# One product for the overflow rows of two grouped quads in a graph network kernel, and their rows summed in bfloat16 parts

## The chip, the cores and the metric

The kernel runs on 1 core of one Trainium2 chip. The metric is the device time of one execution in microseconds; the time before is 2061.96 us, the median of 3 runs (2057.36 to 2062.47).

## What is computed

One layer of a graph network over 6250 nodes of 128 features and 200,000 edges. `f_ij` holds 20 numbers for each edge, `f_ij_cutoff` one.

```
h    = relu(layernorm(x))                       # 6250 x 128
t    = h @ W_in
W_ij = (shifted_softplus(f_ij @ W_f1 + b_f1) @ W_f2 + b_f2) * f_ij_cutoff
x_ij = t[idx_j] * W_ij                          # 200000 x 128; idx_j = dst, sorted
out  = segment_sum(x_ij, idx_i, 6250)           # idx_i = src, in no order
y    = x + shifted_softplus(out @ W_o1 + b_o1) @ W_o2 + b_o2
```

Everything is float32. The time goes to the two large steps: the products that make `x_ij` for 200,000 edges, and the sum of its rows by `src`.

## The kernel before

**Quads.** The edges are cut into chunks of 128, and four chunks make a quad (512 edges); there are 391 quads. One iteration `i` of the main loop works on several quads in different stages. For quad `i-1` TensorE makes `W` (line 494 the bias, line 505 the product), `xg` (line 497, the gathered node rows) and for the quad after next `z` (line 313); ScalarE (ACT) takes exp and ln of z (lines 318 and 323) and scales xg into `xc` (line 510); VectorE (DVE) multiplies W by xc (line 520). This gives the 512 rows of `x_ij`.

**Two ways to sum rows by `src`.** For 223 *plain* and *listed* quads the rows are added to accumulators in HBM by indirect DMAs that add, issued from GpSimd's queue (POOL, line 582, `scatter`), 128 rows each. The tile that holds the rows, `s` (line 519), has four buffers; a quad's buffer is free again when its four scatters have landed. For 168 *grouped* quads TensorE does the sum. The quads 8, 10, 12, 14, 17, 19, 21, 23, ... are grouped (gaps 2, 2, 2, 3), so in nine iterations there are four grouped quads and five others. A grouped quad goes through these steps:

- line 520 writes its rows in float32 into `pt` (`part_new`, line 670, two buffers). `part_rem` (line 676, DVE, iteration q + 2) subtracts twice, so that `pt` holds three parts whose upper halves are bfloat16 (`high`); columns 384 to 386 hold three numbers of the row (`part_ext`, line 682, ACT).
- `perm_oh` (line 662, DVE, iteration q + 1) makes the one-hot matrix `pm` (two buffers), which places each edge into one of 16 groups of 32 slots by its `src`, or, where a group is full, into one of 64 *overflow* slots.
- `permute` (line 687, TensorE, four products `pq` of 128 slots with all 387 columns, each the sum over four chunks) brings the edges to their slots; `perm_out` (line 693, ACT) copies the result to `mst` in bfloat16. Where quad q + 4's iteration holds a unit product, all four are made in iteration q + 3; otherwise two in q + 3 and two in q + 4.
- After eight grouped quads (a round) the *unit product* `un` (lines 761 to 792) adds the rows by node in PSUM, 96 matmuls of 32 rows each, and DVE adds the result to `accT`.

**The overflow.** The 64 overflow slots of a quad are brought together by `over_pe` (lines 702 to 704): per chunk three matmuls of 128 to 131 columns, one for each bfloat16 part, added up in PSUM in float32, twelve matmuls for a quad. The first quad of a pair uses PSUM partitions 0 to 63, the second 64 to 127, each in a PSUM buffer of its own. `over_out` (line 710, ACT) copies the 64 rows to half of the float32 tile `mo` (two of them). When both quads of a pair are there, `over_idx` (line 718) reads each row's node number, `over_dg`, `over_row` and `over_eq` (lines 723, 731, 736) build the matrix `eq` that says which of the 128 rows belong to the same node, `over_sum` (line 741) multiplies it with `mo`, so that every row holds its node's sum, and one scatter adds the result `os` (line 758).

**Order.** Everything is written out by hand: each engine runs its instructions in the program's order. `at(i, point, fn, ...)` hangs a step on a point of iteration i (`L`, `D0`, `D1`, `A0`, `A1`, `DM`, `PE2`, `A2`, `D2`, `S`), and `run` calls them there. `over_pe` hangs on `PE2` behind the products `pq`, for q + 4 (q + 3 where q + 4 is a unit iteration). The PSUM buffers with the tag `B` (four) serve pq, po, the row and sum products, rank products and un. `full[i]` (line 1240) counts the steps in `PE2` that take such a buffer, and moves the copies of a plain quad forward where there are more than two.

**The end.** After the last scatter the accumulators are loaded, added to `accT`, and multiplied by the output weights (lines 1353 to 1430).

Of the kernel before, what the change touches and what calls it, by code (L numbers as in the profile page):

```python
# [7 lines left out]
F32 = mybir.dt.float32  # L8
BF16 = mybir.dt.bfloat16
# [4 lines left out]
ALU = mybir.AluOpType  # L14
# [6 lines left out]
P = 128  # L21
SC = 1024
SEG = 512
GRP = 16
CAP = 32
OVC = 64
# [12 lines left out]
PW = 387  # L39
# [15 lines left out]
def tile_gnn(ctx: ExitStack, tc: tile.TileContext, x, fB, cT, srcT, srcr, dstr, win_, wf1, wf2, bias, bo1c, wo1,  # L55
             wo2, consts, ident, cmap, out, n_edges):
    nc = tc.nc
# [18 lines left out]
    GN = NP // GRP  # L76
# [4 lines left out]
    mpq = sorted_quads(NQ)  # L81
    mpi = {q: n for n, q in enumerate(mpq)}
# [21 lines left out]
    cp = ctx.enter_context(tc.tile_pool(name="cp", bufs=1))  # L104
# [3 lines left out]
    wk = edge.enter_context(tc.tile_pool(name="wk", bufs=2))  # L108
# [41 lines left out]
    dropT = cp.tile([P, EP // P], BF16, name="dropT")  # L150
    mos = []
    for i in range(2):
        mo_ = cp.tile([P, 132], F32, name=f"mo{i}")
        mos.append(mo_)

    rowid = con[:, 0:1]
    wgt = con[:, 1:2]
# [190 lines left out]
    def plainq(q):  # L348
        return q not in mpi and not LB <= plain[q] < LE
# [192 lines left out]
    def s3_idx(q):  # L542
        if not plainq(q):
            return
        s = st[q]["s"]
        jf = sp_.tile([P, 4], F32, tag="jf", name="jf")
        g = plain[q] // 4
        if late.get("jg") != g:
            late["jg"] = g
            late["jd"] = sp_.tile([P, 16], F32, tag="jd", name="jd", bufs=2)  # L550
            n16 = min(16, 4 * NS - 16 * g)
            nc.vector.tensor_scalar(late["jd"][:, :n16], srcT_sb[:, 16 * g:16 * g + n16], trash, None,
                                    op0=ALU.subtract)
        k = 4 * (plain[q] % 4)
        jd = late["jd"][:, k:k + 4]
        nc.vector.scalar_tensor_tensor(jf, s[:, :, 128], wgt2, jd, op0=ALU.is_lt, op1=ALU.mult)
        st[q]["jf"] = jf
# [28 lines left out]
    mp = {}  # L586
# [79 lines left out]
    def high(t):  # L666
        return t.bitcast(BF16)[:, :, 1::2]
# [25 lines left out]
        nc.scalar.copy(mp[q]["ms", s][:, :PW], mp[q].pop(("q", s))[:, :PW])  # L693

    def over_pe(q):
        h = mpi[q] % 2 * OVC
        t = ps.tile([P, 512], F32, tag="B", name="po", bufs=4)
        o = t[h:h + OVC]
        for c in range(4):
            w = mp[q]["pm"][:, c, GRP * CAP:]  # L700
            pt = high(mp[q]["pt"][:, c:c + 1])[:, 0]
            nc.tensor.matmul(o[:, :P + 3], w, pt[:, 2 * P:PW], start=(c == 0), stop=False)  # L702
            nc.tensor.matmul(o[:, :P], w, pt[:, P:2 * P], start=False, stop=False)  # L703
            nc.tensor.matmul(o[:, :P], w, pt[:, :P], start=False, stop=(c == 3))  # L704
        mp[q]["po"] = t

    def over_out(q):
        h = mpi[q] % 2 * OVC
        mo = mos[mpi[q] // 2 % 2]
        nc.scalar.copy(mo[h:h + OVC, :P + 3], mp[q].pop("po")[h:h + OVC, :P + 3])  # L710

    def over_none(q):
        nc.vector.memset(mos[mpi[q] // 2 % 2][OVC:, :P + 3], 0.0)

    def over_idx(q):
        mo = mos[mpi[q] // 2 % 2]
        so = sp_.tile([P, 1], F32, tag="ovs", name="ovs", bufs=3)
        nc.vector.scalar_tensor_tensor(so, mo[:, P + 2:P + 3], float(GN), mo[:, P + 1:P + 2], op0=ALU.mult, op1=ALU.add)
        mp[q]["so"] = so

    def over_dg(q):
# [10 lines left out]
        mp[q]["row"] = t  # L732

    def over_eq(q):
        eq = wk.tile([P, P], F32, tag="oeq", name="oeq", bufs=1)
        nc.vector.tensor_scalar(eq, mp[q].pop("row")[:, :P], mp[q]["so"], None, op0=ALU.is_equal)
        mp[q]["eq"] = eq

    def over_sum(q):
        t = ps.tile([P, 512], F32, tag="B", name="osum", bufs=4)  # L740
        nc.tensor.matmul(t[:, :P + 4], mp[q]["eq"], mos[mpi[q] // 2 % 2][:, :P + 4], start=True, stop=True)
        mp[q]["sum"] = t

    def over_copy(q):
# [91 lines left out]
    with tc.manual_schedule():  # L836
# [98 lines left out]
            nc.vector.tensor_copy(m_[:, :, 128:129], wgt.unsqueeze(1).to_broadcast([P, 4, 1]))  # L935
            ms.append(m_)
        for mo_ in mos:
            nc.vector.tensor_copy(mo_[:, P + 3:P + 4], wgt)
        idl = cp.tile([P, max(NW, 1)], F32, name="idl")
        iotl = cp.tile([P, P + LCAP], F16, name="iotl")  # L940
        nc.vector.tensor_scalar(iotl, iotw[:, GN // 2:GN // 2 + P + LCAP], float(LCAP - 1), None, op0=ALU.subtract)  # L941
# [7 lines left out]
        def at(i, point, fn, *a):  # L949
            hooks.setdefault((i, point), []).append((fn, a))  # L950

        def run(i, point):
            for fn, a in hooks.pop((i, point), []):
                fn(*a)

        at(1 if spread else 0, "D2", rel_ext, 0, rel0)
        if CE < EP // P:
            w = (CE + 4 * NS) // 2
# [145 lines left out]
        for t in range(0, NPT, 4):  # L1104
            i = mid + 8 * (t // 4) if spread else 0
            at(min(i + 9, NQ + 1), "D2", x_bias, t)
        r0_at = 0
        for g in range(len(tgroups)):
            i = clear(max(r0_at + 1, ret_at + 5), units)
# [4 lines left out]
        for r in range(-(-len(mpq) // RKQ)):  # L1114
            i = mpq[RKQ * r]
# [10 lines left out]
        for w in range((LE - LB) // SW):  # L1126
            for g in range(4):
                n = LB + SW * (w - 1) + 4 * g
                i = splain[n] + 2 if w else 6 + 2 * g
# [4 lines left out]
                i = clear(i + 2, units)  # L1134
# [4 lines left out]
            i = clear(i, units)  # L1139
# [4 lines left out]
            i = clear(i + 3, units)  # L1144
            at(i, "PE2", l_place, w)
            at(i + 1, "D0", l_take, w)
            i = clear(wend[w] + 12, units)
# [15 lines left out]
        for q in mpq:  # L1163
            at(q + 1, "D2", perm_oh, q)
            at(q + 2, "D2", part_rem, q, 1)
            at(q + 2, "D2", part_rem, q, 2)
            at(q + 2, "A2", part_ext, q)
            if q + 4 in units:
                for s in range(4):
                    at(q + 3, "PE2", permute, q, s)  # L1170
                for s in range(4):
                    at(q + 3, "PE2", perm_out, q, s)
                at(q + 3, "PE2", over_pe, q)
                at(q + 3, "PE2", over_out, q)
            else:
                for s in range(4):
                    at(q + 3 + s // 2, "PE2", permute, q, s)
                    at(q + 4 + s // 2, "A0", perm_out, q, s)
                at(q + 4, "PE2", over_pe, q)
                at(q + 5, "A0", over_out, q)  # L1180
            if q == mpq[-1] and mpi[q] % 2 == 0:
                at(q + 4, "D2", over_none, q)
            if mpi[q] % 2 or q == mpq[-1]:
                at(q + 5, "DM", over_idx, q)
                at(q + 6, "A0", over_dg, q)
                k = clear(q + 6, units)
                at(k, "PE2", over_row, q)
                at(k + 1, "D0", over_eq, q)
                k = clear(q + 8, units)
                at(k, "PE2", over_sum, q)  # L1190
                at(k + 1, "A0", over_copy, q)
                at(k + 1, "DM", over_ji, q)
                at(k + 1, "A2", over_int, q)
                at(k + 2, "S", over_scatter, q)
# [13 lines left out]
        for i in range(max(NQ + 7, last + 16, r0_end + 2, lend + 24)):  # L1208
            if i % 2 == 0 and i // 2 + 2 <= (NQ - 1) // 2:
                load_sc(i // 2 + 2)  # L1210
            run(i, "L")
            run(i, "D0")
            if i < NQ:
                s1_oh(i)
            run(i, "D1")
            if 0 <= i - 1 < NQ:
                s1_eq(i - 1)
            if 0 <= i - 1 < NQ:
                s2_pe_x(i - 1)
                s2_pe_w(i - 1)  # L1220
            if i + 1 < NQ:
                s1_pe(i + 1)
            if i < NQ:
                s1_exp(i)
                s1_ln(i)
            if 0 <= i - 3 < NQ and not full[i - 1]:
                s3_copy(i - 3, 0)
                s3_copy(i - 3, 1)
            run(i, "A0")
            if 0 <= i - 4 < NQ:  # L1230
                s3_ji(i - 4)
            run(i, "A1")
            if 0 <= i - 1 < NQ:
                s2_copy(i - 1)
            run(i, "DM")
            if 0 <= i - 1 < NQ:
                s2_m(i - 1)
            if 0 <= i - 3 < NQ:
                s3_idx(i - 3)
            full[i] = sum(fn in banked for fn, _ in hooks.get((i, "PE2"), [])) > 2  # L1240
            if 0 <= i - 2 < NQ:
                s3_pe(i - 2)
                if full[i]:
                    s3_copy(i - 2, 0)
                    s3_copy(i - 2, 1)
            run(i, "PE2")
            run(i, "A2")
            run(i, "D2")
            if 0 <= i - 4 < NQ and plainq(i - 4):
                s3_scatter(i - 4)  # L1250
            if 0 <= i - 2 < NQ and i - 2 not in mpi and not plainq(i - 2):
                s3_scatter(i - 2)
            run(i, "S")
# [26 lines left out]
    with tc.For_i(0, trips, 1) as ci:  # L1280
# [51 lines left out]
        eq = wk.tile([P, P], F32, tag="eq", name="feq", bufs=3)  # L1332
# [15 lines left out]
    pt = ctx.enter_context(tc.tile_pool(name="pt", bufs=2, space=PSUM))  # L1348
# [100 lines left out]
def sorted_quads(nq):  # L1449
    qs, q = [], MP0  # L1450
    while q < nq - MPEND:
        qs.append(q)
        q += MPGAPS[(len(qs) - 1) % len(MPGAPS)]
    return qs if len(qs) % RND <= EXTRA else qs[:len(qs) // RND * RND]
# [24 lines left out]
def clear(i, busy, n=1):  # L1479
    while any(i + k in busy for k in range(n)):  # L1480
        i += 1
    return i
# [113 lines left out]
```

## Time and profile before

| | |
|---|---|
| median of 3 runs | 2061.96 us (2057.36 to 2062.47) |
| the profiled execution | 2079.2 us, its span 2077.4 us |
| mean granted TensorE clock | 0.963 |
| TensorE busy | 1862.5 us (90%) |
| VectorE busy | 1659.4 us (80%) |
| GpSimd busy | 1643.9 us (79%) |
| ScalarE busy | 1482.8 us (71%) |
| po, lines 702 to 704 | 3 x 672 matmuls, busy 131.2, 127.2 and 127.3 us |
| pq, line 687 | 2688 matmuls, busy 533.0 us |
| scatters, line 582 | 987, of which 768 take 1.622 us on average |
| mo, line 710 | 168 copies of 0.262 us |
| osum, line 741 | 84 products, 168 float32 passes of 0.295 us |

The profile comes from one execution, recorded by the hardware profiler. Busy time is the time in which an engine has an instruction under way; TensorE's matmuls overlap, so that two of 0.22 us may start 0.06 us apart, and what a matmul costs is read from one start to the next. Behind the bar of a line of the profile stand the busy time, the mean duration of one instruction in ns, and the idle time before the group with what ended it. "issue" is a time in which the engine waited for nothing that the profile shows. POOL is GpSimd, PEld TensorE's weight loads.

### The profile page before, as it was taken

Reading aid. Unit: us, or ns where it says so; the run is one execution under the profiler, and the core shown is the slowest. Engines: PE = TensorE matmul, PEld = TensorE weight load, DVE = VectorE, ACT = ScalarE, POOL = GpSimd, SP = SyncE. Lnnn points to the kernel's source line nnn. Section 1 sums busy time; section 2 is a strip of 40 time slices with the busy share of each in tenths; the row PEclk is TensorE's granted clock in tenths of the full one; section 3 lists DMA queues with packets and bytes.
Section 4 is the critical chain, followed back from the end, with each engine's and each line's share of the span. In section 5 each row is a group of like instructions: output and inputs, shape, how many; then the busy total and the mean of one; then the engine's idle time right before and its main releaser. Section 6 shows DMA issues by size and latency. Waiting matters only on the chain. (4 is left out here: it accounts for less than half of the span.)

```text
span 2077.4 us, 57578 instructions
## 1 busy us (share of the span) xinstructions
PE 1862.5 (90%) x20381; PEld 1288.0 (62%) x20381; DVE 1659.4 (80%) x4448; ACT 1482.8 (71%) x4083; POOL 1643.9 (79%) x1040
## 2 busy tenths in 40 slices
PE   3579988899999999999999999999999999999956
PEld 2456666566666666666666666666666666677734
DVE  3678887797888888988988978979889788787635
ACT  2468776777776777777678777777877777788714
POOL 3578787888877888887878878888888888888774
PEclk9679999999999999999999999999999999999977
DMA  7887766667766766766667666676676676667648
GB/s 238 227 210 147 125 118 120 121 112 130 130 118 114 126 127 119 139 123 123 120 120 130 120 119 118 118 124 117 120 134 108 124 121 111 110 119 131 130 48 239
DMA packets 381188, 272.57 MB, mean 131 GB/s; under 512 B 97727, under 2 KB 341354, under 8 KB 380898
## 3 DMA queue, kind: packets, MB, share of 16 engines
q0 software_dynamic: 143728, 71.30, 35.2%
q1 hardware_dynamic: 236882, 197.50, 34.1%
q8 instruction: 161, 2.64, 0.5%
q14 instruction: 129, 1.06, 0.2%
q10 hardware_dynamic: 288, 0.07, 0.0%
HBM read 154.45 MB, written 114.24 MB: 129 GB/s over the span
## 5 line engine op out<-in xcount | busy, mean ns | idle before, releaser
L582 POOL DMA_INDIRECT acc<-s,lji x768 | 1245.7, 1622 | 266.6 <-issue 180.3
L687 PE MATMUL pq<-pt,pm 128*128 128x387 bf16 x2688 | 533.0, 341 | 44.6 <-DVE pt L676 10.6
L510 ACT ACTIVATE xc<-xg,cb 128x128 f32<-128x128 f32 x1564 | 446.4, 371 | 135.7 <-PE xg L497 119.9
L505 PE MATMUL W<-w,a 128*128 128x128 f32 x3128 | 464.1, 292 | 0.1
L505 PEld LDWEIGHTS W<-w,a 128*128 128x128 f32 x3128 | 388.4, 195 | 42.3 <-issue 3.1
L687 PEld LDWEIGHTS <-pm 128*128 128x128 bf16 x2688 | 260.3, 99 | 233.4 <-issue 37.2
L693 ACT CAST mst<-pq 128x387 bf16<-128x387 f32 x672 | 302.2, 481 | 135.0 <-PE pq L687 96.5
L781 PE MATMUL un<-so,mst 32*128 32x392 bf16 x8064 | 374.5, 327 | 17.3 <-DVE pr L627 7.0
L781 PEld LDWEIGHTS <-mst 32*128 32x128 bf16 x8064 | 227.8, 93 | 157.1 <-issue 60.2
L323 ACT ACTIVATE a<-a,con 128x512 f32<-128x512 f32 x391 | 282.3, 722 | 12.7
L582 POOL DMA_INDIRECT acc<-s,ji x123 | 200.2, 1628 | 80.4 <-issue 26.4
L318 ACT ACTIVATE a<-z 128x512 f32<-128x512 f32 x391 | 238.3, 610 | 26.8 <-PE z L313 17.2
L676 DVE TENSOR_TENSOR pt<-pt 128x512 f32<-128x512 f32 x336 | 231.8, 690 | 5.8
L662 DVE TENSOR_SCALAR pm<-iot,pos 128x576 bf16<-128x576 f16 x672 | 221.8, 391 | 0.0
L792 DVE TENSOR_TENSOR accT<-un,accT 128x392 f32<-128x392 f32 x320 | 158.6, 558 | 73.7 <-PE un L781 37.5
L520 DVE TENSOR_TENSOR s<-W,xc 128x512 f32<-128x512 f32 x192 | 131.9, 687 | 85.9 <-ACT xc L510 52.0
L766 DVE TENSOR_SCALAR so<-iot,mst 128x392 bf16<-128x392 f16 x672 | 191.0, 344 | 6.7 <-PE un L781 6.7
L582 POOL DMA_INDIRECT acc<-os,oji x96 | 156.4, 1629 | 31.2 <-issue 18.0
L497 PE MATMUL xg<-wn,oh 63*128 63x128 bf16 x1564 | 157.3, 222 | 15.8 <-ACT xc L510 9.4
L313 PE MATMUL z<-ft,ws 123*128 123x512 bf16 x391 | 152.0, 389 | 15.7 <-DVE iotl L941 9.4
L494 PE MATMUL W<-b2rep,onesb 64*128 64x512 bf16 x391 | 153.9, 394 | 0.0
L520 DVE TENSOR_TENSOR pt<-W,xc 128x512 f32<-128x512 f32 x168 | 115.2, 686 | 47.9 <-ACT xc L510 29.5
(209 smaller groups left out, 2435.5 us busy)
## 6 DMA issues: line engine op xcount, KB each, us to landing
rb<-reld SPq DMA_DIRECT2D x391, 64.0 KB
fsd<-f SPq DMA_DIRECT2D x49, 480.0 KB
ft<-fsd SPq DMA_DIRECT2D x195, 120.0 KB
sb<-src SPq DMA_DIRECT2D x169, 128.0 KB
fb<-in_fB_dram SPq DMA_DIRECT2D x49, 320.0 KB
ft<-fsd SPq DMA_DIRECT2D x195, 80.0 KB
wn<-tab SPq DMA_DIRECT2D x782, 15.8 KB
acc<-s,lji POOLq DMA_INDIRECT x768
```

The lines of the kernel that those rows point to most:

```text
L318: nc.scalar.activation(a, st[q]["z"], AF.Exp)
L323: nc.scalar.activation(a, a, AF.Ln, bias=half, scale=0.5)
L505: nc.tensor.matmul(W[:, c, :], st[q]["a"][:, c * P:(c + 1) * P], w2, start=False, stop=(c == 3))
L510: nc.scalar.mul(xc[:, c, :], st[q]["xg"][:, c, :], late["c", q // CQ][:, 4 * (q % CQ) + c:4 * (q % CQ) + c + 1])
L520: nc.vector.tensor_tensor(m[:, :, :P], st[q]["W"], st[q]["xc"], op=ALU.mult)
L582: nc.gpsimd.indirect_dma_start(out=accs[k][:rows, :], out_offset=bass.IndirectOffsetOnAxis(ap=ji, axis=0), in_=s, in_offset=None, compute_ ...
L662: nc.vector.tensor_scalar(pm[:, c], iot[:, :SLOTS], rk[r]["pos"][:, 4 * j + c:4 * j + c + 1], None, op0=ALU.is_equal)
L676: nc.vector.tensor_tensor(pt[:, :, k * P:(k + 1) * P], a, high(a), op=ALU.subtract)
L687: nc.tensor.matmul(t[:, :PW], mp[q]["pm"][:, c, s * P:(s + 1) * P], high(mp[q]["pt"][:, c:c + 1, :PW])[:, 0], start=(c == 0), stop=(c == 3))
L693: nc.scalar.copy(mp[q]["ms", s][:, :PW], mp[q].pop(("q", s))[:, :PW])
L766: nc.vector.tensor_scalar(so, iotw[:, :GN], w[:, 3 * P // 2:3 * P // 2 + 1], None, op0=ALU.is_equal)
L781: nc.tensor.matmul(ts[g][:, :GN], mp[q]["ms", s][v, k * P:(k + 1) * P], mp[q]["oh"][v], start=(q == qs[0] and k == 0), stop=(q == qs[-1] a ...
```

## The change

- `mo` becomes bfloat16 and holds the three parts side by side (387 columns, and a column with the row weight).
- `over_pe` handles both quads of a pair in one call: for each chunk one matmul of all 387 columns for the first quad into partitions 0 to 63, then one for the second into partitions 64 to 127, of the same PSUM buffer, eight matmuls for a pair.
- It hangs on a new point, `PE1`, in iteration q + 3 of the pair's second quad. `PE1` is run before the products of a plain quad and before `PE2`. `over_out` follows there: one copy of 128 rows with 387 columns. `over_none` goes into it.
- `over_idx` reads the two columns of `mo` in their new place, `eq` is bfloat16, and `over_sum` makes three matmuls, one for each part, in place of one in float32.
- `over_pe` no longer counts in `full`, since it isn't in `PE2`.
- The scratch memory for the descriptors of GpSimd's DMAs is set to 8192 bytes of a partition; nothing was set before, which means 16384.

In the order of TensorE's instructions the pair's eight products now stand right behind z (line 313) of their iteration. `pt` and `pm` keep two buffers each; those of a pair's first quad are now read until iteration q + 3 of the second.

```diff
-        mo_ = cp.tile([P, 132], F32, name=f"mo{i}")
+        mo_ = cp.tile([P, PW + 1], BF16, name=f"mo{i}")
...
     def over_pe(q):
-        h = mpi[q] % 2 * OVC
+        qs = mpq[mpi[q] // 2 * 2:mpi[q] + 1]
         t = ps.tile([P, 512], F32, tag="B", name="po", bufs=4)
-        o = t[h:h + OVC]
         for c in range(4):
-            w = mp[q]["pm"][:, c, GRP * CAP:]
-            pt = high(mp[q]["pt"][:, c:c + 1])[:, 0]
-            nc.tensor.matmul(o[:, :P + 3], w, pt[:, 2 * P:PW], start=(c == 0), stop=False)
-            nc.tensor.matmul(o[:, :P], w, pt[:, P:2 * P], start=False, stop=False)
-            nc.tensor.matmul(o[:, :P], w, pt[:, :P], start=False, stop=(c == 3))
-        mp[q]["po"] = t
+            for h, p in enumerate(qs):
+                nc.tensor.matmul(t[h * OVC:(h + 1) * OVC, :PW], mp[p]["pm"][:, c, GRP * CAP:],
+                                 high(mp[p]["pt"][:, c:c + 1, :PW])[:, 0], start=(c == 0), stop=(c == 3))
+        mp[q]["po"] = t, len(qs) * OVC
 
     def over_out(q):
-        h = mpi[q] % 2 * OVC
+        t, n = mp[q].pop("po")
         mo = mos[mpi[q] // 2 % 2]
-        nc.scalar.copy(mo[h:h + OVC, :P + 3], mp[q].pop("po")[h:h + OVC, :P + 3])
-
-    def over_none(q):
-        nc.vector.memset(mos[mpi[q] // 2 % 2][OVC:, :P + 3], 0.0)
+        nc.scalar.copy(mo[:n, :PW], t[:n, :PW])
+        if n < P:
+            nc.vector.memset(mo[n:, :PW], 0.0)
...
-        eq = wk.tile([P, P], F32, tag="oeq", name="oeq", bufs=1)
+        eq = wk.tile([P, P], BF16, tag="oeq", name="oeq", bufs=1)
...
     def over_sum(q):
         t = ps.tile([P, 512], F32, tag="B", name="osum", bufs=4)
-        nc.tensor.matmul(t[:, :P + 4], mp[q]["eq"], mos[mpi[q] // 2 % 2][:, :P + 4], start=True, stop=True)
+        mo = mos[mpi[q] // 2 % 2]
+        nc.tensor.matmul(t[:, :P + 4], mp[q]["eq"], mo[:, 2 * P:], start=True, stop=False)
+        nc.tensor.matmul(t[:, :P], mp[q]["eq"], mo[:, P:2 * P], start=False, stop=False)
+        nc.tensor.matmul(t[:, :P], mp[q]["eq"], mo[:, :P], start=False, stop=True)
...
                 for s in range(4):
                     at(q + 3, "PE2", perm_out, q, s)
-                at(q + 3, "PE2", over_pe, q)
-                at(q + 3, "PE2", over_out, q)
             else:
                 for s in range(4):
                     at(q + 3 + s // 2, "PE2", permute, q, s)
                     at(q + 4 + s // 2, "A0", perm_out, q, s)
-                at(q + 4, "PE2", over_pe, q)
-                at(q + 5, "A0", over_out, q)
-            if q == mpq[-1] and mpi[q] % 2 == 0:
-                at(q + 4, "D2", over_none, q)
             if mpi[q] % 2 or q == mpq[-1]:
+                at(q + 3, "PE1", over_pe, q)
+                at(q + 3, "PE1", over_out, q)
                 at(q + 5, "DM", over_idx, q)
...
                 s3_idx(i - 3)
+            run(i, "PE1")
             full[i] = sum(fn in banked for fn, _ in hooks.get((i, "PE2"), [])) > 2
...
-    nc = bacc.Bacc("TRN2", target_bir_lowering=False, num_devices=1)
+    nc = bacc.Bacc("TRN2", target_bir_lowering=False, num_devices=1, dynamic_dma_scratch_size=8192)
```

More of the change, by code (lines that the diff above doesn't have):

```diff
@@ L717, in over_idx @@
         so = sp_.tile([P, 1], F32, tag="ovs", name="ovs", bufs=3)
-        nc.vector.scalar_tensor_tensor(so, mo[:, P + 2:P + 3], float(GN), mo[:, P + 1:P + 2], op0=ALU.mult, op1=ALU.add)
+        nc.vector.scalar_tensor_tensor(so, mo[:, PW - 1:PW], float(GN), mo[:, PW - 2:PW - 1], op0=ALU.mult, op1=ALU.add)
         mp[q]["so"] = so
@@ L937, in tile_gnn @@
         for mo_ in mos:
-            nc.vector.tensor_copy(mo_[:, P + 3:P + 4], wgt)
+            nc.vector.tensor_copy(mo_[:, PW:PW + 1], wgt)
         idl = cp.tile([P, max(NW, 1)], F32, name="idl")
```

## The prediction

> **What bounds the kernel now.** I read the sums of the page first, then busy time by stretch for all engines, then who GpSimd waits for, then the timeline around one overflow product.
>
> ```profile
> PE 1862.5 (90%) x20381; PEld 1288.0 (62%) x20381; DVE 1659.4 (80%) x4448; ACT 1482.8 (71%) x4083; POOL 1643.9 (79%) x1040
> ```
>
> TensorE looks like the bound with 90%, GpSimd (POOL) like an engine with a fifth to spare. The stretches correct that; their columns are the stretch, its length, then busy time and instructions of PE, PEld, DVE, ACT, POOL.
>
> ```profile
> 119.10:330.00 210.90, 189.43 (x1927) 131.13 (x1925) 174.27 (x490) 159.69 (x449) 169.27 (x105) 0.96 0.75 143
> 330.00:1300.00 970.00, 904.76 (x10269) 620.18 (x10271) 822.98 (x2261) 726.87 (x2015) 792.50 (x487) 0.98 0.69 122
> 1300.00:1960.00 660.00, 635.72 (x7160) 441.49 (x7153) 543.74 (x1414) 509.07 (x1410) 552.81 (x344) 1.00 0.69 121
> 1960.00:2017.20 57.20, 40.70 (x530) 27.96 (x528) 28.78 (x84) 15.33 (x49) 46.15 (x30) 0.85 0.47 53
> ```
>
> POOL's instructions here are the row scatters of line 582, and before nearly every one the engine stands 0.30 us on "issue", which is no idleness that another engine could fill:
>
> ```profile
> POOL acc L582 <- issue: 112.3, 368, 0.3
> POOL acc L582 <- DVE s L520: 24.9, 12, 4.7
> POOL acc L582 <- DMA acc<-s,lji: 14.5, 42, 2.0
> ```
>
> (the waits of POOL between 330 and 1300 us). So a scatter occupies 1.62 us and 0.30 us of issue. From 1300 to 1960: 552.8 + 344 x 0.30 = 656 of 660 us. From 330 to 1300: 792.5 + 487 x 0.30 = 939 of 970. TensorE and POOL are both full; of the whole time from 119.1 to 2017.2 us POOL spends 1560.7 + 966 x 0.30 = 1850.5 us of 1898.1, and only 47.6 us on real waits. Of these 10 lie before 330 us (mostly for landed DMAs), 31 between 330 and 1300 (the 12 waits for s of line 520 give 24.9 - 12 x 0.3 = 21), 4 after that and 2 at the last stage. The tail starts from POOL's last scatter: it ends at 2017.1, the loads of the accumulators follow it, and the tail takes 60 us whatever happened before. TensorE is done at 2009.
>
> So **what TensorE saves is worth at most the time that POOL waits for it**, 31 + 4 + 2 less 2 us for landed DMAs (42 x 0.3 of their 14.5 us is issue): some 35 us.
>
> **What the overflow costs TensorE now.** One quad:
>
> ```profile
> 1233.92 0.34 PE L687 MATMUL pq<-pt,pm 128*128 128x387 bf16 x1
> 1234.19 0.25 PE L702 MATMUL po<-pt,pm 128*64 128x131 bf16 x1
> 1234.27 0.22 PE L703 MATMUL po<-pt,pm 128*64 128x128 bf16 x1
> 1234.33 0.22 PE L704 MATMUL po<-pt,pm 128*64 128x128 bf16 x1
> ...
> 1234.87 0.22 PE L704 MATMUL po<-pt,pm 128*64 128x128 bf16 x1
> 1235.02 0.39 PE L494 MATMUL W<-b2rep,onesb 64*128 64x512 bf16 x1
> ```
>
> Starts count here, since matmuls overlap: from the last pq to the next W 1.10 us. Where no po stands between (1229.43, eight pq of 0.34 within 1.57, W at 1230.93) it is 0.27. A quad's overflow costs 0.83 us, 168 quads 139 us. pq to pq is (1.57 - 0.34) / 7 = 0.17, pq to po 0.27: changing to 64 columns costs 0.10 on the way in, and I take as much on the way out.
>
> **What replaces it.** Eight products of 387 columns for two quads, the halves in turn, between z (line 313) and the next full product: 2 x 0.10 for the change of shape, and 0.17 for each product, 8 x 0.17 + 0.20 = 1.56 us, if one follows the other; 4 x 0.17 + 0.20 = 0.88 if the two halves run at once. No row of before shows two column halves at once. The nearest for it is the unit product, four groups of 32 rows at once:
>
> ```profile
> 1236.66 4.16 PE L781 MATMUL un<-so,mst 32*128 32x392 bf16 x96
> ```
>
> 96 products of 392 columns in 4.16 us are 0.043 us each, a quarter of 0.17. The nearest against it are the eight pq in a row. I take 0.88, because un is the row in which products of separate parts of the array alternate as here. A pair then saves 2 x 0.83 - 0.88 = 0.78 us, 84 pairs 65; at 1.56 it saves 0.10, 84 pairs 8.
>
> The weight loads (line 702, 0.11 us each for 64 columns) hide: in the fence of one quad the products start each 0.06 us, with a load each. If they stood bare, a product would cost 0.17 + 0.11, the pair 8 x 0.28 + 0.20 = 2.44 us, and TensorE would lose 0.78 x 84 = 66 us. The Trainium skill (TensorE: Matmul & The Clock Gate, Part 3) says that a weight load overlaps matmuls under way only when the row groups differ, and all eight here use all 128 rows: by that rule this loss is the outcome. The trace of before does not agree: its twelve steps of 0.06 us use the same rows throughout.
>
> *The sum over rows* (line 741): float32, two passes, 0.23 us from 1232.47 to the next pq at 1232.70; now three bfloat16 products of 128 to 132 columns at 0.06 = 0.18. 84 x 0.05 = 4 us saved.
>
> *The place.* The pair's product moves ahead, to iteration q + 3 of the second quad, right behind z. There it needs that quad's remainders (line 676, DVE), which are late in about half of the 84 places: at 1380.05 the two take until 1381.46, while z is done with its place at 1379.68. Before, only pq waited there (until 1381.52), and lcnt, osum or the rank products filled part of that time; now they stand behind the waiting po. Going through the timeline pair by pair, the late remainders cost at most 41 us in all, and what stood in their shadow is 20 to 25. I charge 20. Behind the waiting po on TensorE: the rank, row and sum products, pq and the next iteration.
>
> *The evacuation* (line 710): two of 0.262 us become one like line 693's, 0.481. ACT now waits for it before the next exp, up to about 1 us; exp and ln are needed an iteration (4.8 us) later, and that hides it. Its copies of the second pair of pq come later, though, into the iteration of a unit product, whose four tiles need those PSUM buffers: between nothing and 0.5 us, 42 times, 0 to 20 us; I take 5.
>
> *The second buffer.* pt of a pair's first quad now stays until iteration q + 3, and with two buffers the m of the quad after (line 520, DVE) has to wait for po in every other pair. In those places it starts 1.6 to 6.4 us after W, median 3.5, po ends 2.5 after W. So it costs nothing in most, and at most 1 us where it waits. The bfloat16 eq and the memset are within 0.1 us of what they replace.
>
> *The halved descriptor scratch* of GpSimd's DMAs: no row shows a wait for it. The two ends are the shortest scatter, 1.54 us, at which it costs nothing, and the longest, 2.54, at which 987 scatters cost 987 us; a gain would need a scatter under 1.54, and there is none. I take zero, because 643 of the 963 scatters after 119 us lie within 0.02 of the shortest. Each 0.01 us per scatter would be 10 us, for POOL has no slack to hide it.
>
> Sum on TensorE: 65 + 4 - 20 - 5 = 44 us saved, spread evenly: 23 of them between 330 and 1300 us, and some 5 before, against 29 us of waits on POOL there; after 1300 POOL waits 6 more. I take some seven tenths of the 35, because the waits come in lumps (10 us of them between 600 and 700), ahead of which TensorE has not yet won as much: **25 us**. What is late next is POOL; the rest of TensorE's saving turns into waits of line 520 for the scatter buffers s. The profiled execution took 2079.2 with a span of 2077.4, so its span becomes 2052; the median of the runs is 2062.0, 17 lower, and I subtract from that: 2037.
>
> **The rivals.**
> - *The halves run one after the other.* For it: no row shows the contrary. TensorE saves 8 + 4 and pays 20 + 5 for the place and the evacuation, 13 us lost; the half of it that falls between 330 and 1300 us makes POOL wait longer, the rest is in POOL's stock of rows (at 1810 us a listed quad's scatter starts 11 to 15 us after its line 520): some 2068, and 2054 to 2072 with the bounds of these costs.
> - *Slower: scatters wait for descriptor space.* Place: POOL, line 582. It decides as soon as a scatter takes 25 / 987 = 0.025 us more. The mean is already 0.08 above the shortest; as much again gives 79 - 25: 2116. Against it: most scatters follow each other at 1.54 + 0.30 us without any wait.
> - *Slower: weight loads bare.* TensorE loses 66 - 4 and 20 for the place, all of it on the path: some 2140. Against it: the steps of 0.06 us.
> - *More than POOL's waits:* scatters shorten too, because 74 us of their time is excess over 1.54. By the timeline line 676 (DVE) lies beside the 164 scatters over 1.7 us for 0.55 us on average and beside the others for 0.12; nothing removes it, but its place may shift. 2015 to 2022.
>
> **How the numbers follow.** Forecast (2022 to 2048) 0.65; one after the other 0.14, of which half is slower and a third within 0.3% (6 us, about what a measurement of this kernel can tell from no change); scratch 0.08; bare loads 0.04; more 0.04; unnamed 0.05. The range, 2022 to 2068, leaves out scratch, bare loads, more, and the top of the second case. Faster by over 0.3%: 0.65 + 0.02 + 0.04 less a little, 0.70; within: 0.10; slower: 0.20.
>
> **What would show it.** Right: po starts 0.09 apart on average, eight within 0.9 us; POOL's waits for s shrink from 25 us to a few, its sum of busy and issue reaches 99% from 330 us on; line 520 waits for landed scatters; the last scatter ends near 1992. Wrong: po starts 0.17 apart; mean of line 582 above 1.65 us; TensorE waiting for line 676 over 40 us in all, or un for line 693; POOL still waiting for s.

## The result, and the profile after

The changed kernel takes 2068.98 us (median of 10 runs, 2063.73 to 2075.84) against 2062.82 us (10 runs) of the kernel before beside it: a ratio of 1.0034, 95% interval 1.0018 to 1.0049. It is slower by a third of a per cent. The forecast was 2037 us, a gain, with a range of 2022 to 2068. In a later comparison on another chip (`a_again` below) the change lost 0.2%, and with three buffers (`v6`) as much. The profiled execution took 2067.92 us, its span 2066.1.

The sums of the profile, and busy time by the same stretches as before:

```profile
PE 1815.0 (88%) x19121; PEld 1190.5 (58%) x19121; DVE 1658.7 (80%) x4448; ACT 1468.1 (71%) x3999; POOL 1648.0 (80%) x1040
```

```profile
119.10:330.00 210.90, 186.86 (x1785) 119.33 (x1787) 173.86 (x489) 158.06 (x440) 171.42 (x106) 0.94 0.73 143
330.00:1300.00 970.00, 887.89 (x9683) 576.09 (x9672) 831.86 (x2295) 723.99 (x1988) 802.15 (x491) 0.98 0.67 123
1300.00:1960.00 660.00, 620.22 (x6713) 408.97 (x6716) 540.61 (x1399) 508.20 (x1390) 551.91 (x342) 0.99 0.67 122
```

Between 330 and 1300 us TensorE is busy 17 us less than before (887.9 against 904.8), and that is no gain: it is idle instead. The wait that stands out on TensorE after the change, and one on ScalarE (line, what it waited for, us in all, times, longest):

```profile
PE po L700 <- DVE pt L676: 63.3, 47, 4.0
```

```profile
ACT mo L707 <- PE po L700: 106.3, 83, 4.4
```

In an execution of the kernel before (the run `b_again` below) TensorE's wait for line 676 stood at its pq and was small, and ScalarE waited for single po of one quad, a little each time:

```profile
ACT mo L710 <- PE po L704: 30.2, 96, 0.9
...
PE pq L687 <- DVE pt L676: 9.7, 18, 1.3
```

ScalarE's figure varies between profiles: 106.3 us here, 76.2 in `a_again`, 64.0 in `v6`; TensorE's is 61 to 63 in all three.

One such place after the change, on TensorE, VectorE and ScalarE:

```profile
1238.63 0.38 PE L313 MATMUL z<-ft,ws 123*128 123x512 bf16 x1
1238.94 0.36 PE L700 MATMUL po<-pt,pm 128*64 128x387 bf16 x1
1240.37 0.86 PE L700 MATMUL po<-pt,pm 128*64 128x387 bf16 x7 [1.07 <-DVE pt L676]
1241.16 0.39 PE L612 MATMUL rkp<-G,tri 128*128 128x512 bf16 x1
```

```profile
1237.44 0.46 DVE L599 TENSOR_TENSOR G<-ge 128x512 bf16<-128x512 bf16 x1
1237.82 0.64 DVE L601 TENSOR_REDUCE cnt<-ge 128x32 f32<-128x480 bf16 x1
...
1238.90 1.42 DVE L676 TENSOR_TENSOR pt<-pt 128x512 f32<-128x512 f32 x2
```

```profile
1238.00 1.16 ACT L510 ACTIVATE xc<-xg,cb 128x128 f32<-128x128 f32 x4
1241.26 0.48 ACT L707 CAST mo<-po 128x387 bf16<-128x387 f32 x1 [2.10 <-PE po L700]
```

The first quad's product runs at 1238.94; the second's needs the remainders of line 676, which VectorE begins only after other work at 1238.90, and TensorE stands 1.07 us. ScalarE has reached its copy at 1239.16 and stands 2.10 us, and the next exp and xc stand behind it in its order. GpSimd's waits for the whole stretch from 119.1 to 2017.2 us, after the change:

```profile
POOL acc L582 <- issue: 235.3, 771, 0.4
POOL acc L582 <- DMA acc<-s,lji: 16.6, 46, 1.2
POOL acc L582 <- DVE s L520: 15.7, 14, 2.9
```

and in `b_again`:

```profile
POOL acc L582 <- issue: 227.3, 745, 0.3
POOL acc L582 <- DMA acc<-s,lji: 19.8, 55, 1.1
POOL acc L582 <- DVE s L520: 18.0, 15, 2.8
```

The wait for s that was to shrink to a few us is 15.7, against 18.0 in `b_again` (25.5 in the profile of the prediction): it has hardly changed.

### The profile page after: what moved, and what is told of

Same layout as the page of the kernel before. It is cut to its first block, busy times and chain, and to the rows that moved or that the text cites. A ratio compares the mean times of both kernels' runs of the same rounds, so it can differ in the third digit from the quotient of the medians.

```text
span 2066.1 us, 54971 instructions
## 1 busy us (share of the span) xinstructions
PE 1815.0 (88%) x19121; PEld 1190.5 (58%) x19121; DVE 1658.7 (80%) x4448; ACT 1468.1 (71%) x3999; POOL 1648.0 (80%) x1040
```

## The experiments

The runs stand in four groups, each on one chip of its own beside runs of the kernel before: the first four rows, the next four, then three and three. The kernel before took 2063.9, 2075.1, 2079.2 and 2077.4 us there, so times are compared within a group and only ratios from group to group. The ratio is to the kernel before. "No overflow scatters" and "line 676 a copy" leave out part of the work, so these runs say something of time alone.

| run | what | us | ratio (95%) |
|---|---|---|---|
| b_again | the kernel before | 2063.1 | 1.0000 (0.9984 to 1.0015) |
| b_scratch | before, scratch 8192 | 2063.1 | 1.0007 (0.9991 to 1.0023) |
| b_noos | before, no overflow scatters | 2043.9 | 0.9907 (0.9875 to 0.9939) |
| a_noos | changed, no overflow scatters | 2036.8 | 0.9882 (0.9849 to 0.9916) |
| v1 | changed, later place, pm two buffers | 2079.8 | 1.0024 (1.0005 to 1.0043) |
| a_lateout | changed, ScalarE's copy later | 2129.1 | 1.0267 (1.0240 to 1.0295) |
| a_copy | changed, line 676 a copy | 2051.3 | 0.9899 (0.9871 to 0.9927) |
| b_copy | before, line 676 a copy | 2061.1 | 0.9931 (0.9903 to 0.9958) |
| v6 | changed, three buffers | 2084.3 | 1.0019 (1.0005 to 1.0034) |
| v5 | v6 with the product moved | 2068.0 | 0.9949 (0.9931 to 0.9967) |
| v5_noos | v5, no overflow scatters | 2029.5 | 0.9768 (0.9745 to 0.9790) |
| a_again | changed | 2080.5 | 1.0021 (1.0006 to 1.0037) |
| b_again2 | the kernel before | 2076.5 | 1.0003 (0.9990 to 1.0016) |
| v5_again | v5 | 2066.5 | 0.9954 (0.9940 to 0.9968) |

**1. The kernel before once more, and its scratch.** `b_again` has no edit; `b_scratch` has one line:

```diff
-    nc = bacc.Bacc("TRN2", target_bir_lowering=False, num_devices=1)
+    nc = bacc.Bacc("TRN2", target_bir_lowering=False, num_devices=1, dynamic_dma_scratch_size=8192)
```

> The kernel before, unchanged, for a second profile: the first one's execution took 2079.2 us, 16 more than the median of its runs. Theory A (GpSimd's scatters are full in an ordinary execution, and the first profile shows waits that an ordinary one has not): the span is 2056 to 2066 and GpSimd's real waits (idle beyond 0.305 us before a scatter) from 119 us to the last scatter are about 30 us, as in the profile after (28), against 44 in the first profile. Theory B (the first profile is typical in this, and the change lost TensorE's saving to new waits): the waits are again 40 us or more.

> The kernel before with the descriptor scratch of GpSimd's DMAs at 8192 bytes, nothing else. Theory C (the smaller scratch makes the scatters longer, which is the loss of the change): mean of the list scatters 1.63 us or more against 1.62, and 4 to 10 us slower than before. Theories A and B: within 0.1% of before.

The scratch costs nothing that can be measured, so theory C falls (mean of a listed scatter 1.618 us, `b_again` 1.619). `b_again` shows how much one profile of the kernel before differs from the next: GpSimd's real waits after 119 us (each idle time less 0.305 us of issue) are 28.6 us at 2060.4 us, where the profile of the prediction had 44.0 at 2079.2. That is what theory A expected, on this chip; experiment 7 has a profile of the same kernel with 45.7.

**2. GpSimd relieved.** In both kernels the 84 scatters of the overflow rows are left out:

```diff
-    for q in mpq[1::2] + mpq[-1:] * (len(mpq) % 2):
-        scat[q + 10] += 1
...
-                at(k + 2, "S", over_scatter, q)
```

> The kernel before without the 84 scatters of the overflow rows (their sums are made but not added to the accumulators, so that part is missing in the output). GpSimd has 84 x 1.92 = 161 us less to do and is no longer full. Theory A: the time falls by 20 to 50 us and TensorE alone is the bound. If TensorE and the others were the bound already, it falls by less than 10.

> The changed kernel without the 84 scatters of the overflow rows (that part is missing in the output). Theory A: with GpSimd relieved, TensorE's saving shows: 25 to 45 us below the kernel before without these scatters. Theory B (what TensorE saves in products it loses again by waiting for the remainders of line 676 at the new place): less than 10 us below it, and TensorE's waits for line 676 stay above 40 us.

GpSimd then has some 160 us less to do and waits 186 us (before) and 160 us (changed), yet the time falls by only 19 us (before, by the ratio) and 31 us (changed, from 1.0034 to 0.9882). So the work in order on TensorE, VectorE and ScalarE is a second bound just behind GpSimd. There the change gains 7 us, not 44, and TensorE waits 61.5 us for line 676 in `a_noos` too, as theory B of that expectation has it: most of what is saved in products is lost in waits.

**3. The copy on ScalarE later.** The product stays, its copy goes behind the copies of pq, or to the start of q + 4:

```diff
-                at(q + 3, "PE1", over_out, q)
+                if q + 4 in units:
+                    at(q + 3, "PE2", over_out, q)
+                else:
+                    at(q + 4, "A0", over_out, q)
```

> The changed kernel with only the copy of po on ACT moved: to the copies of pq in a unit case, else to the start of iteration q + 4. ACT then no longer waits 106 us for po ahead of exp and xc; TensorE's products stay where the change put them. Theory A1, TensorE's wait for line 676 (63 us) is what eats the saving: nothing is won, 2064 to 2070. Theory A2, ACT's wait is what does it, because xc of line 510 comes late and line 520 waits for that (120 us before line 520 in the changed kernel, 82 to 120 in the kernel before): 2052 to 2062, and the waits of line 520 for xc fall by 20 us or more.

Neither theory saw this: it is 54 us slower than the kernel before. Two of TensorE's waits:

```profile
PE pq L687 <- ACT mst L693: 35.5, 62, 0.6
...
PE un L780 <- ACT os L745: 15.1, 32, 0.6
```

In the changed kernel these two waits are 3.4 and 0.5 us. By the program's order po now holds one of the four PSUM buffers of tag B while the products pq are made, and both lines are waits for ScalarE to give such a buffer back; that the held buffer is the cause is read from this and not tested by itself. The run doesn't say what ScalarE's 106 us cost, since taking them away brought a worse wait.

**4. The later place, first try.** pt gets three buffers, and the product goes behind pq or, where the next grouped quad is three away, into q + 4:

```diff
-                at(q + 3, "PE1", over_pe, q)
-                at(q + 3, "PE1", over_out, q)
+                if q + 4 in units:
+                    at(q + 3, "PE2", over_pe, q)
+                    at(q + 3, "PE2", over_out, q)
+                elif q + 2 in mpi:
+                    at(q + 3, "PE1", over_pe, q)
+                    at(q + 3, "PE1", over_out, q)
+                else:
+                    at(q + 4, "PE2", over_pe, q)
+                    at(q + 5, "A0", over_out, q)
```

> The changed kernel with the pair's eight products moved to where the old ones stood or later: behind the four products pq in iteration q + 3 where a unit product follows in q + 4, as in the change where the next grouped quad comes two iterations later, and else in iteration q + 4 behind pq, its copy in q + 5; pt gets a third buffer, so that nothing waits for its release. Theory A, the place eats the saving (TensorE waits 63 us for line 676 in the changed kernel, ACT 106 us for po): these two waits fall below 30 and 40 us, the order of the work loses its delay, and the time falls to 2050 to 2060, below both kernels. Theory B, the scatters of line 582 are what lengthened (their sum over 1.54 us each is 80 us against 72, and that sets the end): the waits for line 676 may fall as well, but the time stays at 2064 to 2069 unless that sum falls too. Theory C, the copy of the pair (0.48 us on ACT) is what delays, wherever it stands: 2064 to 2069 with ACT's wait for po gone.

By its time this looks like theory B. Its waits say otherwise: pm still had two buffers, and VectorE, making the next one-hot matrix, stood for po:

```profile
DVE pm L662 <- PE po L700: 67.2, 35, 12.3
```

A wait was exchanged for another (and the sum of the scatters over 1.542 us each, 86.6 us, is the longest of all profiles), so the run decides nothing.

**5. Line 676 with one read.** In both kernels line 676 becomes a copy of the upper halves; the remainders are left out:

```diff
-        nc.vector.tensor_tensor(pt[:, :, k * P:(k + 1) * P], a, high(a), op=ALU.subtract)
+        nc.vector.tensor_copy(pt[:, :, k * P:(k + 1) * P], high(a))
```

> The changed kernel with line 676 made a copy of the upper halves alone, which reads one tile in SBUF where the subtraction reads two; the remainders are left out, so the parts are wrong, and every other instruction stays. It is meant to last about as long (0.5 to 0.7 us). Scatters beside line 676 are longer: those with 0.3 us or more of it beside them exceed the shortest by 0.19 to 0.24 us, those without by 0.05. Theory P, the two reads of VectorE hold up the scatters: the sum over 1.54 us each falls from 80 us to 40 to 50, and with POOL freed by 30 us the time falls to 2045 to 2055. Rival Q, the two only fall in the same stretch of an iteration and the scatters are long for another reason: the sum stays at 70 to 80 us, and the time at 2062 to 2069. If the copy turns out much shorter, TensorE waits less for it, and the sum alone tells them apart.

> The kernel before with the same edit as in the run beside it: line 676 a copy that reads one tile, the remainders left out. Theory P: the sum of the scatters over 1.54 us falls from 72 us to 40 to 50, and the time from 2063 to 2045 to 2055. Rival Q: the sum and the time stay. Between the two kernels: if the change lost its 6 us through longer scatters beside line 676, then without those the changed kernel is as fast as this one or up to 7 us faster (as it was without the overflow scatters); if the loss comes from its place in TensorE's order, the changed kernel stays 5 us or more slower than this one.

```profile
L676 DVE CAST pt<-pt 128x512 f32<-128x512 bf16 x336 | 152.6, 454 | 5.8
```

In `a_copy` it takes 0.454 us where the subtraction takes 0.690, so two things change at once. The scatters' sum over 1.542 us goes to 59 us (changed) and 63.5 (before), less than expected of theory P, but in its direction: scatters with 0.3 us or more of line 676 beside them exceed by 0.12 and 0.13 us, with the subtraction by 0.17 to 0.21 in the ten profiles that have it; the others by 0.04 to 0.06 throughout. The Trainium skill (SBUF — State Buffer, section "SBUF: two separate sides") says that a VectorE operation with two inputs in SBUF and a GpSimd operation that reads SBUF lock each other out for the whole instruction. The traces show longer scatters beside line 676, by 0.2 us on average and not by its 0.69; and beside the copy, which has one input, they are longer by about the same share of its duration (0.12 of 0.454 against 0.19 of 0.690), so that the two inputs are the cause is not shown. The changed kernel is 10 us faster than the one before in this form. By the expectation of `b_copy` that speaks for the scatters and against the place, but the copy doesn't separate the two: with line 676 early, TensorE waits 42 us for it instead of 62 to 63, ScalarE 36 us for po instead of 76 to 106 (the two profiles of the changed kernel), so that the place costs less too.

**6. The place alone.** `v6` is the control: the changed kernel with three buffers for pt and pm (scratch 4096 to make room). `v5` differs from it in this alone:

```diff
-                at(q + 3, "PE1", over_pe, q)
-                at(q + 3, "PE1", over_out, q)
+                if q + 4 in units:
+                    at(q + 3, "PE2", over_pe, q)
+                    at(q + 3, "PE2", over_out, q)
+                else:
+                    at(q + 4, "PE1", over_pe, q)
+                    at(q + 4, "PE1", over_out, q)
```

> The changed kernel with three buffers for pt and for pm in place of two (the scratch for descriptors goes to 4096 bytes to make room), and the pair's product where the change put it. It is the control for the next run, and says what VectorE's waits for po cost (7 us ahead of line 520 in the changed kernel). Theory A, the place: ratio to the kernel before 1.000 to 1.005 as for the changed kernel, the waits for line 676 stay at 55 to 65 us. Rival R, the release of the buffers: ratio 0.990 to 0.997.

> The same three buffers, and the pair's product moved: where a unit product follows in q + 4 behind the products pq of q + 3, else right behind z an iteration later, in q + 4, where line 676 of the pair's second quad has long been done; the copy of po follows at once. Last time, with two buffers for pm, the later place made VectorE wait 67 us for po to release pm, which can't be here. Theory A, the place eats the saving: the waits of TensorE for line 676 fall from 63 us to 15 to 30, ACT's for po from 106 to 40 to 60, and the ratio to the kernel before falls to 0.988 to 0.996 (a part of the 65 us; POOL's waits and scatters hold the rest). Theory B, POOL's scatters alone set the time: ratio 0.998 to 1.004, whatever TensorE waits for. Theory C, the shape of the product itself on TensorE: the ratio stays at 1.000 to 1.005 and TensorE is busy or waits elsewhere for what it saved.

> The run beside it without the 84 scatters of the overflow rows (they are left out, so their rows are missing from the sum). POOL then has 161 us less to do and waits for s throughout, so that the time shows TensorE's order alone. The kernel before gave a ratio of 0.991 in this form, the changed one 0.988. Theory A: 0.965 to 0.980, since the 65 us of TensorE come through but for what VectorE and ScalarE (80% and 71% busy) then hold up. Theories B and C: 0.985 to 0.992, as without the move; by B there is nothing more to win once POOL is free, by C nothing was saved.

`v6` keeps the loss (1.0019) and the wait at po:

```profile
PE po L700 <- DVE pt L676: 61.0, 45, 5.3
```

so the release of the buffers isn't it. `v5` is 16 us faster than `v6`, and 11 us faster than the kernel before. Line 676 is waited for only at pq, somewhat more than expected, and ScalarE's wait for po is 23.4 us, less than expected:

```profile
PE pq L687 <- DVE pt L676: 34.4, 31, 2.2
...
ACT mo L707 <- PE po L700: 23.4, 47, 1.2
```

With GpSimd relieved the ratio is 0.9768 against 0.9907 of the kernel before: TensorE's saving is then worth some 29 us, give or take 8 by the intervals, where the change's own place gave 7. (The two ratios come from two chips, and no run has the three buffers alone in this form.) Theory A holds; B falls (the time moved by 16 us with the place alone) and C falls. This is the version that beats both kernels, the one before by half a per cent and the changed one by 0.7.

**7. All three on one chip.** `a_again`, `b_again2` and `v5_again` have no further edits.

> The changed kernel once more, with its two neighbours on the same chip. Open is on which account its loss stands: against the kernel before, its scatters were 8 us longer in sum (80 against 72 over 1.54 us each) at equal waits (28 us each), from one profile each. Theory A, the place: the time lies 0 to 8 us above the kernel before, 12 to 20 us above the moved version, and POOL's waits are larger than in both; the 8 us of longer scatters do not come again. Rival S, a side effect of the change on the scatters: their sum is 6 us or more above that of the kernel before once more, with waits within 4 us of it.

> The kernel before, unchanged, as the neighbour of the two others: ratio within 0.2% of 1; sum of the scatters over 1.54 us 68 to 76 us and waits 28 to 44 us, which are its two values so far.

> The version with three buffers and the pair's product moved to q + 4 (behind pq in q + 3 ahead of a unit product), once more. Theory A: ratio 0.993 to 0.997, waits for line 676 30 to 40 us, ACT's for po 20 to 30; POOL's waits 8 us or more below those of the changed kernel on this chip. Rival S: its gain stands in shorter scatters, 6 us or more in sum.

The three times repeat, and the waits of `b_again2`, 45.7 us, lie just above the 28 to 44 expected. What each profile gives for GpSimd (real waits, and the sum of the scatters over 1.542 us each, both after 119 us):

| profile | its time | waits | over 1.542 | last scatter ends |
|---|---|---|---|---|
| before | 2079.2 | 44.0 | 75.8 | 2017.1 |
| b_again | 2060.4 | 28.6 | 72.2 | 1998.8 |
| b_again2 | 2075.4 | 45.7 | 70.9 | 2013.8 |
| after | 2067.9 | 28.1 | 80.3 | 2006.8 |
| a_again | 2071.3 | 35.6 | 77.2 | 2009.5 |
| v6 | 2085.3 | 51.9 | 75.3 | 2023.8 |
| v5 | 2068.0 | 37.5 | 72.1 | 2006.1 |
| v5_again | 2060.2 | 26.3 | 74.5 | 1998.9 |

The two sums together follow the end to within 2 us from row to row. That is bookkeeping, since GpSimd's time to its last scatter is made of scatters, issue and waits: it says in which form a loss arrives there, and not what caused it. The profile of `a_again` fell on the shortest of its 12 runs (median 2080.5), so its waits can't be set against those of its neighbours without care; theory A's larger waits than in `b_again2` were not seen. Rival S is half borne out: its 6 us of longer scatters came again (77.2 against 70.9), though the waits differ by 10. What moving the place won stands mainly in the waits (`v6` to `v5`: 14.4 us of 17.7, one profile each, both near the median of their runs).

## Why the prediction was wrong

From the traces, TensorE's time from each start to the next, less idle time, after 119 us:

| us | b_again | b_again2 | after | a_again | v5 | v5_again |
|---|---|---|---|---|---|---|
| po | 139.4 | 140.7 | 87.1 | 88.5 | 69.7 | 69.3 |
| osum | 24.5 | 24.1 | 15.0 | 15.2 | 19.4 | 19.4 |
| all products | 1761.8 | 1768.8 | 1724.9 | 1730.7 | 1724.0 | 1718.5 |
| idle | 105.3 | 115.7 | 151.4 | 148.4 | 151.2 | 150.2 |
| mean granted clock | 0.984 | 0.984 | 0.976 | 0.974 | 0.971 | 0.975 |

The profiles `b_again2`, `a_again` and `v5_again` share a chip; `after` and `v5` are each from another.

- **The price of a quad's overflow, 0.83 us or 139 in all:** right, 139.4.
- **The pair's price, 0.88 us, halves at once:** right. Where po doesn't wait, the pair takes 0.82 us from its first start to the next product, and the step from z ahead of it is 0.09 longer (0.31 us, against 0.22 from z to a product of 128 columns), 0.91 in all. The eight products last 0.34 us each and take 0.89 together, in `v5`:

```profile
1242.82 0.89 PE L700 MATMUL po<-pt,pm 128*64 128x387 bf16 x8
1243.64 0.39 PE L494 MATMUL W<-b2rep,onesb 64*128 64x512 bf16 x1
```

- **Weight loads hide:** right; eight loads of 0.11 us lie inside those 0.82 us, on the same rows throughout. The rule of the Trainium skill that was weighed there (TensorE: Matmul & The Clock Gate, Part 3) would have given 2.44 us for a pair; the trace does not agree with it.
- **Sum over rows, 4 us:** 9 by the table; right in sign, a small term.
- **The place, charged at 20 us: the step that failed.** "the late remainders cost at most 41 us in all, and what stood in their shadow is 20 to 25. I charge 20." Measured were 63.3 us of waits, 54 more than in `b_again`. On top of it, a po that is interrupted costs more than its wait: 37 pairs that don't wait take 0.82 us, the other 47 take 1.2 beside the wait, 17 us more in all. So TensorE saved 37 and 38 us of products in the two pairs of neighbours (1761.8 to 1724.9, 1768.8 to 1730.7) and not 69, and got 46 and 33 us more idle time. What failed was to price the places one by one on the old timeline, as if only the waiting product moved. As a reading of that timeline the 41 us were fair. Count as late the time by which line 676 ends after TensorE could start po, 0.31 us behind the start of z: the profile before then has 38 us in 40 of the 84 places, and `b_again` and `b_again2` have 35 and 37. In the changed kernel the same places are late by 78 us, in 49 of them, and in `a_again` by 79. The lateness doubled with the change itself; by what is open.
- **ScalarE's stop at po**, put at "up to about 1 us" each and hidden, was 106 us in 83 places, and 2.10 in the one shown. Whether it delays the rest is not shown, and one reading speaks against much of it: VectorE's waits for xc ahead of line 520 (tiles s and pt) are 119.7 us against 120.5 in `b_again`, and 80.8 in `a_again` against 72.0 in `b_again2`.
- **The other products, taken as unchanged: they cost 25 us more** (of 61.8 us saved on po and osum, 36.9 are left in the sum). Some 7 are z's longer step to po. About 12 go with the granted clock, which the forecast left out: over whole executions it was 0.952 to 0.963 in all runs of the changed kernel and 0.962 to 0.970 in the runs of the kernel before in the four groups. Its trace has the clock at half for 90 us after 119 us, against 62 in `b_again` (99 against 61 in the second pair); taking half of the product time in there as lost, an estimate, gives 33 us against 21 for these products. `a_noos` and `b_noos` bear this out: there the clock hardly differs (0.986 and 0.984 after 119 us), and the other products differ by 7 us, po and osum saving 60 and idle time growing by 36. Why the clock was granted less in the complete kernel is not shown; fewer products alone don't do it.
- **What the later place changed, in TensorE's own account:** not the idle time, which is 150 us in `v5_again` as in `a_again` (148), and the clock is no better. The products are 12 us less, of which po, no longer interrupted, gives 19. From `v6` (1738.1 us of products, 158.1 idle) to `v5` 14 us stand in products and 7 in idle time. That the place costs 16 us is shown by these two runs; by which chain of waits on TensorE, VectorE and GpSimd it reaches the end stays open.
- **What GpSimd could gain, 25 of 35 us:** read from an execution 17 us longer than the median, and 15 of these 17 us were GpSimd's waits (44.0 against 28.6). The working took the difference between profile and median for a mere shift, and it stood in the very term that bounds the gain. With 15 us fewer waits the same seven tenths of the rest are 14 us and not 25, so this alone made the forecast 11 us too good, without changing its sign. (On the chip of the last group, where the kernel before takes 2077 us, it has 45.7 us of waits: they differ between executions or chips, and which of the two isn't shown.)
- **What is late next is GpSimd:** right as far as it went. Without the overflow scatters the moved version wins 29 us, with them 11. But GpSimd never became full: it still waits 26 to 38 us in `v5`.
- **The second buffer of pt:** right for the change (7.3 us of waits, and with three buffers nothing is won). For a later place it was wrong to think of pt alone: pm has the same life.
- **The halved scratch at nothing:** right.
- **Evacuation, 5 us for the unit product:** too much by 5; among TensorE's waits after the change un has none for line 693.
- **What would show it:** "TensorE waiting for line 676 over 40 us" was the sign that came. None of the rivals was the one that happened; it lay in a term of the forecast itself that was given a bound of 41 and should have been a rival of its own. The first rival's "some 2068" is the measured time by luck: its condition, one half after the other, did not come.

What stays open is why the scatters of the changed kernel are 6 to 8 us longer in sum than in the kernel before in both pairs of neighbours. Scatters beside line 676 make up a part of every kernel's excess, and the time that it lies beside them is the same in `b_again` and after (190.5 and 190.7 us).

## What to carry to other kernels

A product that saves time where it stands can lose it where it is moved: ahead of a late operand, the in-order queue behind it pays. A timeline of before gives the lateness of before; the change can make the operand later. Price the move by itself, by a run that differs in the place alone, and give every operand of the later place a buffer for its whole life before drawing a conclusion from it. Before a gain is capped by the waits of the bound engine, read those waits from an execution near the median, or from two.

## What the runs showed of the hardware

- Two products of 64 columns on all 128 rows, one for each half of the PSUM partitions, start 0.003 us apart and run together: eight of 387 columns in 0.82 us, against 0.17 us from one full product to the next, with a weight load of 0.11 us each on the same rows inside that time. The forecast had taken an even 0.09.
- Scatters beside line 676 are longer: by 0.17 to 0.21 us on average with 0.3 us or more of the subtraction beside them (1.3 at most), by 0.12 and 0.13 with the shorter copy, by 0.04 to 0.06 without.
- The complete kernel with fewer products was granted a lower TensorE clock: 0.976 and 0.974 after 119 us against 0.984, and 0.971 and 0.975 in `v5`. Without the overflow scatters it was not lower (`a_noos` 0.986, `b_noos` 0.984), and what lowers it was not tested.
- 84 scatters less, some 160 us of GpSimd's time, were worth only 19 to 38 us (`b_noos`, and `v5_noos` against `v5`): an engine with some 30 us of waits had others close behind it.
